# Sums over features in quarters of the array's columns, and layer 0's broadcast on ScalarE, in a four-layer graph network

## The chip, the cores and the metric

The kernel runs on one core of a Trainium2 chip. The metric is the device time of one execution in microseconds (us), as the median of several runs. The profile is of one further execution. Five engines work side by side: TensorE multiplies matrices (the profile shows its matmuls as PE and its weight loads as PEld), VectorE (DVE), ScalarE (ACT) and GpSimd (POOL) work elementwise, and SyncE (SP) starts most transfers.

## The reference, cut to what matters

The input x has 128 graphs of 64 nodes with 256 features. Four layers follow one another, each a graph operation, then a residual and a layer norm over the features:

```python
x = _layernorm(x + _L0_gnn_ref(x, adj, W, a))             # attention over all pairs of nodes
x = _layernorm(x + _L1_gnn_ref(x, ..., src, dst))         # attention over 512 listed edges
x = _layernorm(x + _L2_gnn_ref(x, adj, ...))              # neighbours' mean, two matmuls, batch norms
x = _layernorm(x + _L3_gnn_ref(x, adj, ...))              # two graph convolutions, four LSTMs
```

The change concerns layers 0 and 1. Layer 0 computes for each pair of nodes e = s1[i] + s2[j], leaky ReLU, a mask, softmax, and a product with Wh. Layer 1 is:

```python
Xq = (H @ W_lin.T).reshape(bt, n, h, dh)                  # 4 heads of 64 features
e = jnp.einsum('behd,hd->beh', leaky_relu(Xq[:, src] + Xq[:, dst], 0.2), a)
e = e + jnp.log(A0[src, dst] + EPS)
m = segment_max(e, src); ex = exp(e - m[src]); attn = ex / segment_sum(ex, src)[src]
Y = segment_sum(attn * Xv[:, dst], src) @ W_out.T
```

For every graph, edge and head, the sum over 64 features of a times a leaky ReLU is the heavy part: 128 x 512 x 256 values go through it. The kernel writes the leaky ReLU as a linear part and a plain ReLU, and folds the absolute value of a into the weights, so that only the sign of a is left to be applied after the ReLU.

## The kernel before, in words

Nodes are taken 512 at a time in 16 blocks q, each of four chunks c of 128 rows, which is two graphs (halves s) per chunk. A step b of a block, of which there are eight, is one graph: b = 2c + s. Two blocks share one softmax S (BPS = 2): 16 graphs with 4 heads give 64 rows of 512 edges.

`l1_graph(q, b)` gathers with a matmul: z, two chunks k of 128 features by 512 edges, is the sum of the queries at an edge's two ends. ScalarE makes u = ReLU(z) (line 324). An order of features was chosen in which feature p of chunk 0 and feature p of chunk 1 belong to the same head; line 325 on VectorE adds the second to the first, times `same`, the product of their signs. `reduce_heads` (line 312) then sums over the 128 partitions: its weights, cut out of `apad`, are zero but for four columns, which hold the signs of the four heads; where the cut begins decides which four of the 128 rows of the PSUM bank e receive this graph. All other rows get zeros added. A list `pend` keeps two steps between ReLU and sum.

`l1_softmax(S)` adds the linear part (line 335, weights `spads`) and the logarithm, and finds maxima and sums over edges with the same source by scans along the edges, which are sorted: a scan to the right and one to the left, the larger of the two, exponential, again two scans. TensorE transposes the result, GpSimd scatters it with four indirect transfers into a table in HBM (line 363), and SyncE loads it back as dense matrices, `ld` (line 369). `v_a` copies it into `am` on GpSimd (line 377) and multiplies it with the values v in 64x64 pieces (line 384); `v_b` applies W_out, the residual and the layer norm; `v_c` multiplies by the normalised adjacency, the start of layer 2.

Layer 0 is `l0_a` (transposes), `l0_b` (matmul with W and with two columns for s1 and s2, then the broadcast `sb` of s2 on GpSimd, line 227), `l0_c` (transposes of `sb`, lines 233 to 247), `l0_d` and `l0_e`.

The written order is one loop over q and b: each step runs `l1_graph` and then pieces of other blocks from a table `between`, layer 0 two blocks ahead (q + 2) and the values three behind (`LAG`). It is no final order: the framework is a planner, which goes by dependences, priorities in written order and its own costs, and may put an instruction of a later step ahead on an engine's queue. On the engine the queue is then followed in order. A tile with `bufs=n` has n buffers, and its writer waits until the readers of the oldest are done. PSUM has eight banks: two z of two banks each, one e, three m for everything else.

After the loop come layer 2 (from line 649) and layer 3 with its LSTMs (from line 790). Of the edits, only the helper `layernorm` (lines 84 to 97) is used there.

Of the kernel before, what the change touches and what calls it, by code (L numbers as in the profile page):

```python
# [17 lines left out]
P = 128  # L18
NB = 128
N = 64  # L20
# [11 lines left out]
SROWS = BPS * GQ * HEADS  # L32
PAIRS = N * N
# [7 lines left out]
def kernel(ctx: ExitStack, tc: tile.TileContext, i, out):  # L41
# [42 lines left out]
    def layernorm(dst, src, n, engine):  # L84

        st = small.tile([P, n, 6], F32, name="ln_st", bufs=6)
        mv = small.tile([P, n, 2], F32, name="ln_mv", bufs=6)
        ng = small.tile([P, n], F32, name="ln_ng", bufs=6)
        rs = small.tile([P, n], F32, name="ln_rs", bufs=6)
        for r in range(n):  # L90
            nc.vector.bn_stats(st[:, r, :], src[:, r, :])
            nc.vector.bn_aggr(mv[:, r, :], st[:, r, :])
        rsqrt(rs, mv[:, :, 1], n)
        nc.vector.tensor_scalar_mul(ng, mv[:, :, 0], -1.0)  # L94
        for r in range(n):
            engine.tensor_scalar(dst[:, r, :], src[:, r, :], ng[:, r:r + 1], rs[:, r:r + 1],
                                 op0=OP.add, op1=OP.mult)
# [13 lines left out]
    with ExitStack() as two:  # L111
# [52 lines left out]
        for k in range(KD):  # L164
            for m in range(KD):
                nc.scalar.dma_start(
                    wq[:, k, m * P:(m + 1) * P].rearrange("p (h j) -> p h j", h=HEADS),
                    i["W_linT"][k * P:(k + 1) * P].rearrange("p (h m j) -> p m h j", h=HEADS, m=KD)[:, m])
        aL1 = su.tile([P, D], F32, name="aL1")
        for m in range(KD):  # L170
            nc.scalar.dma_start(aL1[:, m * P:(m + 1) * P].rearrange("p (h j) -> p h j", h=HEADS),
                              i["L1_gnn_a"].rearrange("h (m j) -> m h j", m=KD)[m].partition_broadcast(P))
# [4 lines left out]
        apad = wa.tile([P, 2 * P - HEADS], F32, name="apad")  # L177
        same = wa.tile([P, 1], F32, name="same")
# [37 lines left out]
        def l0_b(q):  # L216
            xT = L0[q]["xT"]
            wh = L0[q]["wh"] = own(q, [P, PQ, D + 2], "wh")
            for c in range(PQ):
                p_ = bank([D + 2])  # L220
                for k in range(KD):
                    nc.tensor.matmul(p_, xT[:, k, c * P:(c + 1) * P], w0[:, k, :],  # L222
                                     start=k == 0, stop=k == KD - 1)
                nc.scalar.activation(wh[:, c, :], p_, AF.Copy)

            sb = L0[q]["sb"] = own(q, [P, PQ, P], "sb")
            nc.gpsimd.tensor_copy(sb, wh[:, :, D + 1:].to_broadcast([P, PQ, P]))

        def l0_c(q):
            wh, sb = L0[q]["wh"], L0[q]["sb"]  # L230
            sc = bank([PQ, P])
            for c in range(PQ):
                nc.tensor.transpose(sc[:, c, :], sb[:, c, :], ident)
            t = own(q, [P, PQ, P], "lr")
            for c in range(PQ):
                nc.vector.scalar_tensor_tensor(t[:, c, :], sc[:, c, :], wh[:, c, D:D + 1], mask,
                                               op0=OP.add, op1=OP.add)
            e = L0[q]["e"] = work.tile([P, PQ, P], F32, name="e0")
            nc.vector.scalar_tensor_tensor(e, t, SLOPE, t, op0=OP.mult, op1=OP.max)
            mx = small.tile([P, PQ], F32, name="mx")  # L240
            nc.vector.tensor_reduce(mx, e, AX.X, OP.max, negate=True)
            sm = small.tile([P, PQ], F32, name="sm")
            for c in range(PQ):
                nc.scalar.activation(e[:, c, :], e[:, c, :], AF.Exp, bias=mx[:, c:c + 1],
                                     accum_out=sm[:, c:c + 1])
            ri = L0[q]["ri"] = small.tile([P, PQ], F32, name="ri")
            nc.vector.reciprocal(ri, sm)
# [32 lines left out]
        def l1_qv(q, c2):  # L280
            xT, v = L1[q]["xT"], L1[q]["v"]
            sp = spads[q // BPS % 2].rearrange("p (s b c h) -> p s b c h", s=4, b=BPS, c=PQ)
            pv = bank([2, D])
            for c in (2 * c2, 2 * c2 + 1):
                pq = bank([D + HEADS])
                for k in range(KD):
                    nc.tensor.matmul(pq, xT[:, k, c * P:(c + 1) * P], wq[:, k, :],  # L287
                                     start=k == 0, stop=k == KD - 1)
                for k in range(KD):
                    nc.tensor.matmul(pv[:, c % 2, :], xT[:, k, c * P:(c + 1) * P], wv[:, k, :],  # L290
                                     start=k == 0, stop=k == KD - 1)

                qs = work.tile([P, 2, D], F32R, name="qs", bufs=6)
                L1[q]["qs"].append(qs)
                for s in range(2):
                    r, ro = slice(s * N, (s + 1) * N), slice((1 - s) * N, (2 - s) * N)
                    nc.scalar.activation(qs[r, s, :], pq[r, :D], AF.Copy)  # L297
                    nc.vector.tensor_sub(qs[ro, s, :], pq[r, :D], qs[r, s, :].bitcast(F32))  # L298
                    nc.scalar.activation(sp[r, s, q % BPS, c, :], pq[r, D:], AF.Copy, scale=SLOPE)
# [5 lines left out]
        def reduce_heads(q, b, t):  # L305
            S = q // BPS
            c, s = divmod(b, 2)
            r0 = ((s * BPS + q % BPS) * PQ + c) * HEADS
            first = q % BPS == 0 and b == 0
            if first:  # L310
                pes[S] = bank([E], name="e", bufs=1)
            nc.tensor.matmul(pes[S], apad[:, P - HEADS - r0:2 * P - HEADS - r0], t, start=first, stop=False)  # L312

        def l1_graph(q, b):

# [5 lines left out]
            u = work.tile([P, KD, E], F32, name="u", bufs=4)  # L323
            nc.scalar.activation(u, z, AF.Relu)  # L324
            nc.vector.scalar_tensor_tensor(u[:, 0, :], u[:, 1, :], same, u[:, 0, :], op0=OP.mult, op1=OP.add)  # L325
            pend.append((q, b, u[:, 0, :]))
            if len(pend) > DEEP:
                reduce_heads(*pend.pop(0))

        ld = {}  # L330

        def l1_softmax(S):
# [7 lines left out]
            nc.vector.tensor_tensor_scan(up, seg[:, :E], e, NEG, OP.add, OP.max)  # L340
            nc.vector.tensor_tensor_scan(dn[:, ::-1], seg[:, 1:][:, ::-1], e[:, ::-1], NEG, OP.add, OP.max)
            nc.vector.tensor_max(up, up, dn)
            nc.vector.tensor_sub(e, e, up)
            nc.scalar.activation(e, e, AF.Exp)


            nc.vector.tensor_tensor_scan(up, keep, e, 0.0, OP.mult, OP.add)
# [9 lines left out]
            nc.vector.reciprocal(rd, rows[1][:, :, :SROWS])  # L357
            for c in range(EC):
                nc.vector.scalar_tensor_tensor(at[:, c, :], rows[0][:, c, :SROWS], count[:, c:c + 1], rd[:, c, :],
                                               op0=OP.mult, op1=OP.mult)  # L360
# [11 lines left out]
        def v_a(q):  # L372
            S, b = divmod(q, BPS)
            v = L1[q]["v"]
            am = vp.tile([P, PQ * HEADS, N], F32, name="am", bufs=2)
            w = PQ * HEADS
            nc.gpsimd.tensor_copy(am, ld[S][:, :, b * w:(b + 1) * w].rearrange("p n r -> p r n"))
            pY = [bank([KD, PQ, N]) for _ in range(2)]
            for c in range(PQ):
                for h in range(HEADS):  # L380
                    for s in range(2):
# [3 lines left out]
                                         am[r, c * HEADS + h, :], start=True, stop=True)  # L385
# [4 lines left out]
        def v_b(q):  # L390
# [10 lines left out]
            x2 = L1[q]["x2"] = vp.tile([P, PQ, D], F32, name="x2")  # L401
# [81 lines left out]
        acol = su.tile([P, KD], F32, name="acol")  # L483

        def setup_queries():

            tmp2 = su.tile([P, KD, D], F32, name="tmp2")
            nc.vector.tensor_mul(tmp2, wq[:, :, :D], aL1[:, None, :].to_broadcast([P, KD, D]))
            for k in range(KD):
                nc.vector.reduce_sum(wq[:, k, D:], tmp2[:, k, :].rearrange("p (m h j) -> p h m j", m=KD, h=HEADS),  # L490
                                     axis=AX.XY)
            for m in range(KD):
                nc.vector.tensor_mul(tmp2[:, m, :P], aL1[:, m * P:(m + 1) * P], ident)
                nc.vector.reduce_sum(acol[:, m:m + 1], tmp2[:, m, :P], axis=AX.X)
# [4 lines left out]
        def setup_signs():  # L499

            nc.vector.tensor_scalar(acol, acol, 0.0, -2.0, op0=OP.is_lt, op1=OP.mult)
            nc.vector.tensor_scalar_add(acol, acol, 1.0)
            nc.vector.tensor_mul(same, acol[:, 0:1], acol[:, 1:2])
            nc.vector.tensor_scalar_mul(apad, iota_e[:, :2 * P - HEADS], 0.0)
            for h in range(HEADS):
                r, c0 = slice(h * 32, (h + 1) * 32), P - HEADS + h
                nc.vector.tensor_copy(apad[r, c0:c0 + 1], acol[r, 0:1])
# [115 lines left out]
        for q in range(NQ):  # L623
# [11 lines left out]
            for b in range(GQ):  # L635
                some(l1_graph, q, b)
                if q and q % BPS == 0 and b == DEEP - 1:
                    l1_softmax(q // BPS - 1)
# [4 lines left out]
        while pend:  # L643
            reduce_heads(*pend.pop(0))
        l1_softmax(NQ // BPS - 1)
        ph.close()

# [405 lines left out]
```

## Time and profile before

| | us |
|---|---|
| median of 3 runs | 2236.68 (2236.19 to 2237.63) |
| span of the profiled execution | 2237.3 |
| TensorE matmuls busy | 2163.4 |
| TensorE weight loads busy | 1411.7 |
| VectorE busy | 926.0 |
| ScalarE busy | 944.6 |
| GpSimd busy | 435.0 |

The page gives the busy time of each engine, the same in 40 slices of 55.9 us as digits (9 means 90% or more), the chain of work that ended last, and groups of instructions by line: tiles, shape, count, busy time, mean of one in ns, and the idle time ahead of them with what ended it. The busy time of a group counts overlapping instructions once, and matmuls overlap, since one begins while the one before drains. The start-to-start distance tells what a matmul costs. Line 312 appears as 256 instructions for 128 matmuls, because an fp32 matmul is two. Granted clock of TensorE in this execution: 0.991.

### The profile page before, as it was taken

What the parts mean: (1) busy time and instruction counts of PE and PEld (TensorE: products, weight loads), DVE (VectorE), ACT (ScalarE), POOL (GpSimd) and SP (SyncE); (2) the same over time, 40 slices, a digit from 0 to 9 for tenths busy, and PEclk for the clock granted to TensorE, in tenths of its full rate; (3) what the DMA queues carried; (4) which work ended last, traced back from release to release, by engine and by line L of the source; (5) the groups of instructions that cost most, each with busy time, mean ns of one, the idle gap of its engine ahead of it and who ended that gap; (6) DMA issues with size and microseconds to landing.
All of it is one profiled execution on the core that took longest, in us unless ns stands there. A gap on an engine that the chain in (4) does not pass through costs nothing.

```text
span 2237.3 us, 27559 instructions
## 1 busy us (share of the span) xinstructions
PE 2163.4 (97%) x10675; PEld 1411.7 (63%) x10675; DVE 926.0 (41%) x2136; ACT 944.6 (42%) x1821; POOL 435.0 (19%) x561
## 2 busy tenths in 40 slices
PE   5989999999899998999999999999999999999998
PEld 4667676666554444468468468468468468568467
DVE  7576756666544435232232323323323323323212
ACT  2655665656334802343343333333433433433333
POOL 1133334333320002011111111112112112112002
PEclk8999999999999998999999999999999999999999
DMA  4021233202223003000000000001001001000001
GB/s 121 19 40 29 50 50 51 50 32 39 41 41 111 19 0 104 0 20 29 29 20 29 29 19 29 29 20 29 29 19 29 28 20 29 19 10 29 10 0 29
DMA packets 129266, 74.46 MB, mean 33 GB/s; under 512 B 84976, under 2 KB 119920, under 8 KB 128880
## 3 DMA queue, kind: packets, MB, share of 16 engines
q1 hardware_dynamic: 124528, 70.74, 13.0%
q8 instruction: 84, 1.38, 0.3%
q10 hardware_dynamic: 3584, 0.92, 0.2%
q0 software_dynamic: 1024, 1.05, 0.2%
q14 instruction: 46, 0.38, 0.1%
HBM read 44.12 MB, written 28.57 MB: 32 GB/s over the span
## 4 chain that ended last, share of the span: by engine, by line
PE 81%; DVE 9%; ACT 5%; POOL 2%; DMA 1%; issue 1%; ACTq 0%; SPq 0%; POOLq 0%; DVEq 0%
PE l L927 34%; PE l L933 19%; PE pz L749 5%; PE pz L684 4%; DVE u L325 3%; PE g L867 2%; PE g L879 2%; PE e L312 2%; PE m L287 2%; PE m L222 2%; PE m L398 1%; PE g L829 1%; ACT u L324 1%; PE m L410 1%; PE m L290 1%
## 5 line engine op out<-in xcount | busy, mean ns | idle before, releaser
L927 PE MATMUL l<-H,wih 128*128 128x256 f32 (+2 forms) x2496 | 792.7, 470 | 0.8 <-ACT gate_g L947 0.5
L927 PEld LDWEIGHTS l<-H,wih 128*128 128x128 f32 x2496 | 467.7, 190 | 273.7 <-issue 179.4
L933 PE MATMUL l<-hid,whh 128*128 128x256 f32 (+2 forms) x1536 | 435.9, 437 | 0.0
L933 PEld LDWEIGHTS l<-hid,whh 128*128 128x128 f32 x1536 | 291.9, 190 | 128.4 <-issue 61.2
L939 ACT ACTIVATE gate_i<-l,bias 128x256 f32<-128x256 f32 (+2 forms) x176 | 100.0, 568 | 522.7 <-PE l L933 468.7
L942 DVE TENSOR_TENSOR gate_i<-gate_i,gate_g 128x256 f32<-128x256 f32 (+2 forms) x96 | 47.8, 498 | 580.8 <-ACT gate_g L939 580.8
L943 POOL TENSOR_TENSOR cell<-gate_f,cell 128x256 f32<-128x256 f32 (+2 forms) x96 | 83.6, 871 | 903.8 <-ACT gate_f L939 903.8
L82 POOL TENSOR_TENSOR ln_rs<-ln_rs,mhalf 128x2 f32<-128x2 f32 (+2 forms) x97 | 79.5, 819 | 498.7 <-DVE ln_ng L94 497.6
L324 ACT ACTIVATE u<-z 128x1024 f32<-128x1024 f32 x128 | 129.5, 1024 | 59.4 <-PE z L322 58.8
L312 PE MATMUL e<-u,apad 128*128 128x512 f32 x256 | 133.1, 606 | 11.3 <-DVE u L325 9.9
L939 ACT ACTIVATE gate_g<-l,bias 128x256 f32<-128x256 f32 (+2 forms) x176 | 100.1, 569 | 99.1 <-PE l L927 49.9
L325 DVE SCALAR_TENSOR_TENSOR u<-u,same 128x512 f32<-128x512 f32 x128 | 106.3, 841 | 57.8 <-ACT u L324 56.9
L939 ACT ACTIVATE gate_o<-l,bias 128x256 f32<-128x256 f32 (+2 forms) x176 | 99.2, 564 | 64.1 <-PE l L933 54.1
L946 DVE TENSOR_TENSOR cell<-gate_i,gate_g 128x512 f32<-128x512 f32 (+2 forms) x80 | 48.3, 603 | 156.1 <-ACT gate_g L939 155.6
L947 ACT ACTIVATE gate_g<-cell 128x256 f32<-128x256 f32 (+2 forms) x176 | 89.9, 511 | 52.9 <-DVE cell L946 38.4
L684 PE MATMUL pz<-A,w 128*128 128x512 f32 x256 | 112.1, 594 | 0.0
L322 PE MATMUL z<-gath_r,qs 128*128 128x512 f32 x256 | 106.9, 499 | 0.5 <-DVE qs L298 0.3
L684 PEld LDWEIGHTS pz<-A,w 128*128 128x128 f32 x256 | 48.1, 190 | 56.4 <-issue 54.3
L952 DVE TENSOR_TENSOR H<-gate_o,gate_g 128x512 f32<-128x512 f32 (+1 forms) x64 | 40.9, 639 | 89.0 <-PE l L927 71.4
L298 DVE TENSOR_TENSOR qs<-m,qs 64x256 fp32r<-64x256 f32 x128 | 54.1, 423 | 54.9 <-ACT qs L297 53.3
L939 ACT ACTIVATE gate_f<-l,bias 128x256 f32<-128x256 f32 (+2 forms) x96 | 51.0, 531 | 59.7 <-PE l L933 59.7
L287 PE MATMUL m<-wq,tT 128*128 128x260 f32 x256 | 71.2, 396 | 3.7 <-ACT tT L202 3.2
(240 smaller groups left out, 2674.8 us busy)
## 6 DMA issues: line engine op xcount, KB each, us to landing
xin<-in_x SPq DMA_DIRECT2D x16, 512.0 KB
ld<-table SPq DMA_DIRECT2D x16, 512.0 KB
x_dram<-x SPq DMA_DIRECT2D x16, 512.0 KB
x2r<-x_dram SPq DMA_DIRECT2D x32, 256.0 KB
x_dram<-A SPq DMA_DIRECT2D x64, 128.0 KB
x3r<-x_dram SPq DMA_DIRECT2D x64, 128.0 KB
out<-st SPq DMA_DIRECT2D x64, 128.0 KB
wih<-in_WihT SPq DMA_DIRECT2D x3, 1024.0 KB
```

Source lines behind the costliest of these rows:

```text
L287: nc.tensor.matmul(pq, xT[:, k, c * P:(c + 1) * P], wq[:, k, :], start=k == 0, stop=k == KD - 1)
L312: nc.tensor.matmul(pes[S], apad[:, P - HEADS - r0:2 * P - HEADS - r0], t, start=first, stop=False)
L322: nc.tensor.matmul(z[:, k, :], L1[q]["qs"][c][:, s, k * P:(k + 1) * P], gath_r, start=True, stop=True)
L324: nc.scalar.activation(u, z, AF.Relu)
L325: nc.vector.scalar_tensor_tensor(u[:, 0, :], u[:, 1, :], same, u[:, 0, :], op0=OP.mult, op1=OP.add)
L684: nc.tensor.matmul(p_, w1[:, k, m * P:(m + 1) * P], A[:, q, k * QT:(k + 1) * QT], start=k == 0, stop=k == KD - 1)
L749: nc.tensor.matmul(p_, w2[:, k, m * P:(m + 1) * P], hidden(q, k), start=k == 0, stop=k == M1 - 1)
L927: nc.tensor.matmul(gates[n], wih[p][:, k, mw * P:(mw + 1) * P], Hw[:, k, :, s, :], start=k == 0, stop=not s and k == KD - 1)
L933: nc.tensor.matmul(gates[n], whh[p][:, k, m * P:(m + 1) * P], hid[:, k], start=False, stop=k == KD - 1)
L939: nc.scalar.activation(act[n], gates[n], AF.Tanh if n == "g" else AF.Sigmoid, bias=bias[:, p - 1, m:m + 1])
L943: nc.gpsimd.tensor_tensor(cell[:, j], act["f"], cell[:, j], OP.mult)
L947: nc.scalar.activation(act["g"], cell[:, j], AF.Tanh)
```

## The change

Six edits are made.

1. The sum over features takes both chunks k on TensorE, so `same` and line 325 go, and the features stay in their natural order (the four strided loads of `wq` and two of `aL1` become one each). The weights in `apad` are now 32 columns wide (CG) and there is one set per chunk. Each matmul writes to 32 partitions of e only, a quarter of the columns of the array. Graphs are summed in fours, whose quarters n differ, in the order chunk, then the four from the youngest to the oldest. It is meant to let four sums run beside one another in four parts of the array.
2. The broadcast of s2 in layer 0 goes from GpSimd to ScalarE, and e of layer 0 is worked in place.
3. In softmax, the scan to the left runs over the result of the scan to the right, so that the maximum of the two is no longer needed, and the second half (sums, transposes, table) is a function of its own that is called one step later.
4. The layer norm subtracts the mean instead of adding its negative.
5. The rows of e have another order, by quarter, then softmax half; unused rows lie between them, and the reads of softmax, table and `am` follow it.
6. Buffers: u has 7 instead of 4, `am` 1 instead of 2, x2 shares the tile of y.

The core of the diff:

```diff
         for r in range(n):
-            engine.tensor_scalar(dst[:, r, :], src[:, r, :], ng[:, r:r + 1], rs[:, r:r + 1],
-                                 op0=OP.add, op1=OP.mult)
+            engine.tensor_scalar(dst[:, r, :], src[:, r, :], mv[:, r, 0:1], rs[:, r:r + 1],
+                                 op0=OP.subtract, op1=OP.mult)
...
-            nc.gpsimd.tensor_copy(sb, wh[:, :, D + 1:].to_broadcast([P, PQ, P]))
+            nc.scalar.activation(sb, wh[:, :, D + 1:].to_broadcast([P, PQ, P]), AF.Copy)
...
-        def reduce_heads(q, b, t):
+        def reduce_heads(four):
+            q, b, _ = four[0]
             S = q // BPS
...
-            nc.tensor.matmul(pes[S], apad[:, P - HEADS - r0:2 * P - HEADS - r0], t, start=first, stop=False)
+            for k in range(KD):
+                for q, b, u in reversed(four):
+                    n, r0 = b % 2 * 2 + b // 2 % 2, (q % BPS * 2 + b // 4) * HEADS
+                    nc.tensor.matmul(pes[S][n * CG:(n + 1) * CG, :],
+                                     apad[:, k, CG - HEADS - r0:2 * CG - HEADS - r0], u[:, k, :],
+                                     start=r0 == 0 and k == 0, stop=False)
...
-            u = work.tile([P, KD, E], F32, name="u", bufs=4)
+            u = work.tile([P, KD, E], F32, name="u", bufs=7)
             nc.scalar.activation(u, z, AF.Relu)
-            nc.vector.scalar_tensor_tensor(u[:, 0, :], u[:, 1, :], same, u[:, 0, :], op0=OP.mult, op1=OP.add)
-            pend.append((q, b, u[:, 0, :]))
-            if len(pend) > DEEP:
-                reduce_heads(*pend.pop(0))
+            pend.append((q, b, u))
+            if len(pend) == 4 + DEEP:
+                reduce_heads([pend.pop(0) for _ in range(4)])
...
             nc.vector.tensor_tensor_scan(up, seg[:, :E], e, NEG, OP.add, OP.max)
-            nc.vector.tensor_tensor_scan(dn[:, ::-1], seg[:, 1:][:, ::-1], e[:, ::-1], NEG, OP.add, OP.max)
-            nc.vector.tensor_max(up, up, dn)
-            nc.vector.tensor_sub(e, e, up)
+            nc.vector.tensor_tensor_scan(dn[:, ::-1], seg[:, 1:][:, ::-1], up[:, ::-1], NEG, OP.add, OP.max)
+            nc.vector.tensor_sub(e, e, dn)
             nc.scalar.activation(e, e, AF.Exp)
+            sm[S] = e, up, dn
+
+        def l1_weights(S):
+            e, up, dn = sm.pop(S)
...
-                if q and q % BPS == 0 and b == DEEP - 1:
-                    l1_softmax(q // BPS - 1)
+                if q and q % BPS == 0 and b in (DEEP - 1, DEEP):
+                    (l1_softmax, l1_weights)[b - DEEP + 1](q // BPS - 1)
...
-        while pend:
-            reduce_heads(*pend.pop(0))
+        reduce_heads(pend)
         l1_softmax(NQ // BPS - 1)
+        l1_weights(NQ // BPS - 1)
```

## The prediction

> **What bounds the kernel now.** I read the page first (busy rows and slices), then the groups, then single stretches of the timeline. The first 600 us hold the stages that the edits touch; after about 680 us nothing edited runs except the layer norm helper.
>
> ```profile
> PE 2163.4 (97%) x10675; PEld 1411.7 (63%) x10675; DVE 926.0 (41%) x2136; ACT 944.6 (42%) x1821; POOL 435.0 (19%) x561
> ...
> PE   5989999999899998999999999999999999999998
> ...
> L324 ACT ACTIVATE u<-z 128x1024 f32<-128x1024 f32 x128 | 129.5, 1024 | 59.4 <-PE z L322 58.8
> L312 PE MATMUL e<-u,apad 128*128 128x512 f32 x256 | 133.1, 606 | 11.3 <-DVE u L325 9.9
> ...
> L325 DVE SCALAR_TENSOR_TENSOR u<-u,same 128x512 f32<-128x512 f32 x128 | 106.3, 841 | 57.8 <-ACT u L324 56.9
> ```
>
> See that TensorE is the busy engine nearly everywhere, and that the pair of lines to be changed (L312 on TensorE, L325 on VectorE) holds 133 us and 106 us of busy time. The durations of matmuls overlap, so I count starts instead. In the chain, 128 fp32 instructions of 512 columns take 54.94 us, 0.429 us each:
>
> ```profile
> 684.11 54.94 PE pz L684 x128
> ```
>
> and in the timeline, where graph steps follow one another with nothing between:
>
> ```profile
> 583.24 1.03 PE L322 MATMUL z<-gath_r,qs 128*128 128x512 f32 x2
> 584.11 1.02 PE L312 MATMUL e<-u,apad 128*128 128x512 f32 x2
> 584.56 1.03 PE L322 MATMUL z<-gath_r,qs 128*128 128x512 f32 x2
> ...
> 589.90 1.12 PE L312 MATMUL e<-u,apad 128*128 128x512 f32 x2 [0.81 <-DVE u L325]
> ```
>
> A step takes 1.32 us from z to z: 0.86 for the two instructions of e, so 0.46 for the two of z.
>
> Two blocks q (one softmax) repeat every 70.8 us in the middle of the stage:
>
> ```profile
> 261.40:332.20 70.80, 68.41 (x428) 49.93 (x427) 46.94 (x111) 42.92 (x95) 26.04 (x28) 1.00 0.27 47
> ```
>
> The columns are TensorE, weight loads, VectorE, ScalarE, GpSimd, granted clock, DMA. Of the 428 matmuls, 32 are e (32 x 0.429 = 13.7 us). Counting all others at 0.429 us per 512 fp32 columns (transposes of 128 at the 0.109 us between their starts, z at 0.46 a pair) gives 51.6 us. So TensorE streams for 65.3 us and truly stalls for about 5.5 us: the stage is TensorE-bound, and ScalarE (43) and VectorE (47) have room.
>
> What it waits for between 100 and 600 us, in the waits view:
>
> ```profile
> PEld e L312 <- DVE u L325: 20.4, 26, 3.5
> PEld m L233 <- POOL sb L227: 10.2, 11, 2.6
> PEld m L353 <- DVE dn L348: 7.6, 7, 1.2
> PEld e L312 <- DVE e L337: 4.1, 7, 1.0
> ```
>
> All four are waits that the edits touch.
>
> **What the Trainium skill says.** "TensorEngine Tiling (Array Packing)", Key Properties: tiles "can execute LdWeights and Matmul in parallel", and a change of tiling mode drains TensorE. "TensorE: Matmul & The Clock Gate", Measured speedup vs the span model: three tiles of 32 columns with 512 moving columns ran 2.38 times as fast, within about 5 ns of the model of concurrent tiles. No 32-column tile is in this trace; the nearest thing is the 64x64 matmuls of L384, and they agree:
>
> ```profile
> 306.25 0.38 PE L222 MATMUL m<-w,tT 128*128 128x258 f32 x1
> 306.56 1.16 PE L384 MATMUL m<-am,v 64*64 64x64 f32 x64
> 307.65 0.50 PE L322 MATMUL z<-gath_r,qs 128*128 128x512 f32 x1
> ```
>
> Sixty-four fp32 instructions of 218 ns in 1.16 us are (1.16 - 0.22)/63 = 15 ns apart. One after the other they would be 0.429 x 64/512 = 54 ns apart: 3.6 of 4 tiles run at once, although each matmul is two instructions on the same tile. The drain: the last 128-wide stream ends at about 306.47 (306.25 + 0.22), z really begins at about 307.75 (its record is 0.10 longer than usual), so 1.28 us for 16 x 0.054 = 0.86: some 0.4 us per burst.
>
> **The change part by part.**
>
> (1) Column quarters. Before: 128 matmuls, 256 instructions, 256 x 0.429 = 109.8 us. After: 32 calls of 8 matmuls, 16 instructions each. With four tiles at once, 4 x 0.429 = 1.72 us plus 0.4 us of mode change = 2.12 us a call, 67.8 us in all: **42 us less** on the bounding engine. Bounds: perfect without drain 54.9 (55 less); no concurrency 32 x (6.86 + 0.4) = 232 us (123 more). I take four at once, because L384 shows it in this kernel.
>
> (2) L325 goes: 106 us of VectorE. It is off the path where TensorE is busy, and on it in two places. Near a softmax the scans of 1.2 us stand ahead of it on VectorE's queue and e waits; at the end of the loop (588 to 593 us) two of them take 4.2 us and TensorE waits some 3 us. e now waits for ScalarE's ReLU alone, still two steps old when it is used, and the call takes the youngest of its four first, so one wait serves all. The bank of e is next written four steps later than now, so its wait for L337 ends. I count **1 us in each of 7 softmaxes and 3 us at the end: 10 us**.
>
> (3) Layer 0's broadcast moves from GpSimd (0.61 us, behind whatever GpSimd waits for) to ScalarE directly behind the copies that it reads: 16 x 0.6 = 10 us for an engine busy 43 of 70.8 us. The transposes L233 wait 10.2 us for it in 11 cases, partly hidden by the preceding matmul's stream; I take **3 us**.
>
> (4) Softmax: one maximum (0.68 us of VectorE x 8) goes; the second scan now runs over the result of the first. The second half is emitted one step later, so TensorE's transposes L353 stand behind more work and the 1 us each that they wait (7.6 in 7) is covered: **up to 7 us, I take 3**. What waits instead is the table's round trip, treated below.
>
> (5) The negated mean (L94, 0.17 us) goes from every layer norm; GpSimd's power waits for it. Where TensorE is bound this is hidden by its queue; the last normalisation is exposed: 0.2 us, nothing. Layer 0's e in place, x2 in y and one am buffer: hidden by TensorE's work, as a block lies between two uses.
>
> (6) Start: six strided weight loads on ScalarE's queue become two. ScalarE's first copy now waits for these issues until 8.8 us; TensorE's L222 starts at 10.77 but needs VectorE's L419 (to 10.25), so that alone is worth 0.5. VectorE idles 1.9 us for aL1 at 12.9 and then runs without a gap to about 26, with four operations (0.29, 0.28, 0.55, 0.27 us) that go: **3 us** of 60.
>
> Sum: 42 + 10 + 3 + 3 + 3 = 61, less 3 us because ScalarE's copies meet the ReLUs of back-to-back steps (a step would be 0.46 + 0.53 = 0.99 us on TensorE, under ReLU's 1.02, so ScalarE limits these stretches): **58 us**. 2236.7 - 58 = **2179 us**.
>
> **The rivals.**
>
> *Round trip of the table, 2204.* The add of softmax starts at 266.27; the first am of GpSimd ends at 302.9, 36.6 us later; TensorE uses it at 306.56. GpSimd already waits:
>
> ```profile
> POOL am L377 <- DMA ld<-table: 63.6, 7, 11.7
> ```
>
> If the 70.8 us shrink by 6.6, TensorE arrives 36.5 us after the add instead of 40.3. The chain loses 0.7 (maximum) and some five L325 of 0.75, to 32 us, but the later second half can add l0_b, v_a and a step (about 6 us): 38, or 42.6 without that relief. So the table is 1.5 to 6 us late, 3.6 in the middle, in 7 pairs: +25. For it: the slack is small. Against: VectorE is freer, and the written order is only a wish, since the planner already runs graph steps ahead while a softmax is under way (z and e by turns from 263 to 275 us).
>
> *Nearly all stalls go, 2158.* The 5.5 us per pair fall to 2.3 instead of the 3.9 that the sum above leaves (13 us in 8 pairs), and of the drain 0.25 us hides behind weight loads (32 x 0.25 = 8 us): -21. For it: freer VectorE. Against: waits move to other engines rather than vanish.
>
> *Tiles overlap by halves only, 2247.* If the first instruction of a tile waits behind both of the tile before, 8 matmuls take 9 slots: 9 x 0.429 + 0.4 = 4.26 us a call, 136 in all, +27, less 16 from (2) to (6): +11. Against: L384's 15 ns. *No overlap at all, 2343:* +123 - 16. For both: four tiles share all 128 rows here, while the 64x64 ones share only halves.
>
> **How the numbers follow.** Forecast 0.62, round trip 0.15, stalls gone 0.12, halves 0.06, no overlap 0.05. The range 2156 to 2207 holds the first three with the unknown sizes in them (drain 0.2 to 0.5 us a call, stalls) and leaves out most of the last two. Faster 0.89, same 0.01, slower 0.10.
>
> **What would show it.** Right: L312's successor has 512 instructions whose starts come in fours a few ns apart, groups 0.43 us apart; the pair of blocks takes about 64 us; waits of e are on ScalarE's u, small; VectorE about 110 us less; layer 2 begins about 57 us earlier and everything after 700 us is unchanged. Wrong: starts 0.43 us apart singly or in twos; GpSimd's wait for ld showing up as TensorE's wait for am; ScalarE full in the loop.

## The result and the profile after

The changed kernel takes 2257.74 us (median, 2255.42 to 2259.17), the kernel before 2236.76 beside it: a ratio of 1.0092 with a 95% interval of 1.0075 to 1.011. It is **slower by 0.9%**, where 2.6% faster was forecast. The profiled execution has a span of 2253.6 us.

Start with two lines of the page of the changed kernel: busy time of the engines, and the shares of the chain of work that ended last.

```profile
PE 2143.3 (95%) x10931; PEld 1388.0 (62%) x10931; DVE 812.4 (36%) x1898; ACT 952.4 (42%) x1837; POOL 568.7 (25%) x545
...
PE 74%; issue 10%; POOL 9%; DVE 4%; ACT 2%; DMA 1%; POOLq 0%; SPq 0%; ACTq 0%; DVEq 0%
```

VectorE lost 113.6 us of busy time, about what was forecast. The surprise is GpSimd: it should have lost the broadcast of layer 0 and gained nothing, and its busy time rose from 435.0 to 568.7 us. It is only 25% busy, yet the chain runs through it for 9% of the span. Its groups on the page say why:

```profile
L95 POOL TENSOR_SCALAR A<-xin,ln_mv,ln_rs 128x256 f32<-128x256 f32 x64 | 82.1, 1292 | 1.7
...
L95 POOL TENSOR_SCALAR A<-x2r,ln_mv,ln_rs 128x256 f32<-128x256 f32 x64 | 77.8, 1225 | 3.3
L95 POOL TENSOR_SCALAR y<-y,ln_mv,ln_rs 128x256 f32<-128x256 f32 x64 | 77.5, 1220 | 1.7
```

These are three of the four layer norms, 64 normalisations each: layer 0's, the one at the end of layer 2, and layer 1's. One normalisation takes 1.22 us and more (second number after the bar). The first two of these groups in the kernel before:

```profile
L96 POOL TENSOR_SCALAR A<-xin,ln_ng,ln_rs 128x256 f32<-128x256 f32 x64 | 64.2, 1016 | 1.7
L96 POOL TENSOR_SCALAR A<-x2r,ln_ng,ln_rs 128x256 f32<-128x256 f32 x64 | 38.1, 605 | 3.3
```

Layer 1's group has 588 ns there. Layer 0's mean of 1016 ns mixes two lengths: four of its normalisations in a row took 6.01 us at 266.51 us and 2.16 us at 306.91. What makes some of them slow in the kernel before is not shown.

TensorE's sums, on the other hand, look as intended. The timeline of the changed kernel around one call:

```profile
306.63 1.92 PE L309 MATMUL e<-u,apad 128*32 128x512 f32 x16
308.48 0.74 PE L318 MATMUL z<-gath_r,qs 128*128 128x512 f32 x2
```

The z instructions are those of the next graph step. Sixteen instructions on tiles of 32 columns lie in 1.85 us from the start of e to the start of z. Their single starts come in fours 7 ns apart, at 306.63, 307.08, 307.51 and 307.94: four quarters run at once, each four 0.43 us after the one before.

Where the span went, by the times (us) at which stages begin in the traces. The third and fourth kernels are experiments from below: the changed kernel with the norm of before, and that one with the second half of softmax a step later.

| | before | after | norm of before | and softmax later |
|---|---|---|---|---|
| first graph step (z) | 54.5 | 49.3 | 49.3 | 49.0 |
| layer 2 begins | 599.2 | 580.2 | 553.9 | 543.1 |
| LSTMs begin | 884.9 | 879.5 | 839.7 | 828.8 |
| last input matmul of the LSTMs | 2223.6 | 2238.4 | 2178.4 | 2167.5 |
| end | 2237.3 | 2253.6 | 2192.2 | 2181.3 |
| layer 2 to the end | 1638.1 | 1673.4 | 1638.3 | 1638.2 |

Layers 0 and 1 became 19 us shorter, a third of the forecast, and everything after them became 35 us longer, though nothing but the layer norm was touched there.

### The profile page after: what moved, and what is told of

Read it like the earlier page. It is cut to its first block, busy times and chain, and to the rows that moved or that the text cites. A ratio compares the mean times of both kernels' runs of the same rounds, so it can differ in the third digit from the quotient of the medians.

```text
span 2253.6 us, 27724 instructions
## 1 busy us (share of the span) xinstructions
PE 2143.3 (95%) x10931; PEld 1388.0 (62%) x10931; DVE 812.4 (36%) x1898; ACT 952.4 (42%) x1837; POOL 568.7 (25%) x545
## 4 chain that ended last, share of the span: by engine, by line
PE 74%; issue 10%; POOL 9%; DVE 4%; ACT 2%; DMA 1%; POOLq 0%; SPq 0%; ACTq 0%; DVEq 0%
PE l L920 30%; PE l L926 18%; PE pz L742 5%; POOL A L95 3%; PE pz L677 3%; PE g L860 2%; PE g L872 2%; POOL y L95 2%; PE z L318 2%; PE e L309 2%; PE m L398 2%; POOL ln_rs L83 2%; PE m L281 1%; PE g L822 1%; PE m L284 1%
## 5 line engine op out<-in xcount | busy, mean ns | idle before, releaser
L920 PE MATMUL l<-H,wih 128*128 128x256 f32 (+2 forms) x2496 | 798.9, 473 | 0.8 <-ACT gate_g L940 0.5
L920 PEld LDWEIGHTS l<-H,wih 128*128 128x128 f32 x2496 | 470.0, 191 | 277.8 <-issue 183.5
L320 ACT ACTIVATE u<-z 128x1024 f32<-128x1024 f32 x128 | 128.6, 1024 | 34.7 <-PE z L318 34.1
L318 PE MATMUL z<-gath_r,qs 128*128 128x512 f32 x256 | 101.6, 478 | 4.9 <-ACT u L320 4.8
L95 POOL TENSOR_SCALAR A<-xin,ln_mv,ln_rs 128x256 f32<-128x256 f32 x64 | 82.1, 1292 | 1.7
L95 POOL TENSOR_SCALAR st<-x3r,ln_mv,ln_rs 128x256 f32<-128x256 f32 x64 | 77.9, 1226 | 3.4
L95 POOL TENSOR_SCALAR A<-x2r,ln_mv,ln_rs 128x256 f32<-128x256 f32 x64 | 77.8, 1225 | 3.3
L95 POOL TENSOR_SCALAR y<-y,ln_mv,ln_rs 128x256 f32<-128x256 f32 x64 | 77.5, 1220 | 1.7
```

What stands on the lines that cost most here:

```text
L95: engine.tensor_scalar(dst[:, r, :], src[:, r, :], mv[:, r, 0:1], rs[:, r:r + 1], op0=OP.subtract, op1=OP.mult)
L318: nc.tensor.matmul(z[:, k, :], L1[q]["qs"][c][:, s, k * P:(k + 1) * P], gath_r, start=True, stop=True)
L920: nc.tensor.matmul(gates[n], wih[p][:, k, mw * P:(mw + 1) * P], Hw[:, k, :, s, :], start=k == 0, stop=not s and k == KD - 1)
```

## The experiments

### Is it the norm? (four runs)

**The norm of before in the changed kernel** (ln_st gets four buffers instead of six, for room):

```diff
-        st = small.tile([P, n, 6], F32, name="ln_st", bufs=6)
+        st = small.tile([P, n, 6], F32, name="ln_st", bufs=4)
+        ng = small.tile([P, n], F32, name="ln_ng", bufs=6)
+        nc.vector.tensor_scalar_mul(ng, mv[:, :, 0], -1.0)
-            engine.tensor_scalar(..., mv[:, r, 0:1], rs[:, r:r + 1], op0=OP.subtract, op1=OP.mult)
+            engine.tensor_scalar(..., ng[:, r:r + 1], rs[:, r:r + 1], op0=OP.add, op1=OP.mult)
```

> The changed kernel with the layer norm of before (dense negated mean, add then multiply on GpSimd; statistics buffers 4 instead of 6 for room). Theory A, the norm is all of it: GpSimd's operation back from 1.22 to about 0.6 us, the time near the forecast, 2180 to 2195 us. Theory B, the norm costs only what is lost after 600 us (about 28 us of LSTMs, start of layer 3 and layer 2), and the other loss is the planner's order of the sums and the table's round trip: about 2230 us.

Measured: 2195.22 us (2194.0 to 2196.06), ratio to before 0.9804 (0.9788 to 0.982). With this one edit undone, the change is a gain of 2%.

**The norm of the change alone in the kernel before** (the same diff the other way round, nothing else):

> The kernel before with only the layer norm's edit. Theory A: slower by the 28 us seen after layer 1 plus what GpSimd loses in the first 600 us, 2265 to 2290 us; an LSTM group takes 174 instead of 170.4 us. Theory B: 2265 us, nearly all of it after 600 us. Third theory, the LSTM part is longer for another reason (order of the queues): 2237 us.

Measured: 2301.86 us (2299.67 to 2303.7), ratio 1.0277 (1.026 to 1.0295). So the edit costs 62.5 us in the changed kernel (2257.74 - 2195.22) and 63 in the one before (2301.86 - 2238.69).

The edit does two things: it subtracts instead of adding, and it reads the mean with a stride out of the pair (mean, variance) instead of from a dense tile. The next two runs separate them.

**Subtract, from a dense copy of the mean:**

```diff
+        nc.vector.tensor_copy(ng, mv[:, :, 0])
-            engine.tensor_scalar(..., mv[:, r, 0:1], rs[:, r:r + 1], op0=OP.subtract, op1=OP.mult)
+            engine.tensor_scalar(..., ng[:, r:r + 1], rs[:, r:r + 1], op0=OP.subtract, op1=OP.mult)
```

> As the changed kernel, subtract then multiply, but the mean is first copied to a dense tile. If the operation subtract is what takes 1.22 us on GpSimd, it stays 1.22 us and the time about 2258 us. If reading the mean with a stride of two elements is what costs, it takes 0.6 us and the time is that of the run with the add back.

Measured: 2260.09 us, ratio 1.0089 (1.0072 to 1.0106).

**Add, with the mean negated in place and read with a stride:**

```diff
+        nc.vector.tensor_scalar_mul(mv[:, :, 0], mv[:, :, 0], -1.0)
-            engine.tensor_scalar(..., mv[:, r, 0:1], rs[:, r:r + 1], op0=OP.subtract, op1=OP.mult)
+            engine.tensor_scalar(..., mv[:, r, 0:1], rs[:, r:r + 1], op0=OP.add, op1=OP.mult)
```

> As the changed kernel, but the mean is negated in place and added, read with a stride of two elements. If the operation subtract costs: 0.6 us each and the time of the run with the add back. If the stride costs: 1.22 us each and about 2258 us.

Measured: 2194.93 us, ratio 0.9803 (0.9786 to 0.9819). ln_st has its six buffers here, so their number doesn't matter either. One and the same group of GpSimd's normalisations from the first, third and fourth of these kernels:

```profile
L97 POOL TENSOR_SCALAR A<-x2r,ln_ng,ln_rs 128x256 f32<-128x256 f32 x64 | 38.2, 608 | 3.3
```
```profile
L97 POOL TENSOR_SCALAR A<-x2r,ln_ng,ln_rs 128x256 f32<-128x256 f32 x64 | 77.8, 1225 | 3.3
```
```profile
L96 POOL TENSOR_SCALAR A<-x2r,ln_mv,ln_rs 128x256 f32<-128x256 f32 x64 | 38.1, 605 | 3.3
```

Rows with the same tiles but another operation differ by a factor of two (608 and 1225 ns); rows with the same operation and another source of the mean don't (608 and 605; and 1225 dense against 1225 in the changed kernel). **It is the operation**, not the stride. In layer 0 the two operations differ less, 718 and 1292 ns. Why GpSimd takes longer to subtract, no run shows.

### How an idle engine costs 62 us

GpSimd waits far more than it works, so its longer instructions must stand in somebody's way. The chain of work of the changed kernel at the start of an LSTM group (start, length, what):

```profile
1229.08 0.73 POOL ln_rs L83
1229.89 2.43 POOL st L95 x2
...
1235.26 0.96 POOL A L95
1236.47 1.22 POOL A L95
...
1238.69 2.44 POOL A L95 x2
1241.17 0.46 PE g L822 x16
1241.63 7.04 PE l L920 x12
```

Three norms of two rows (st is the last norm of one group's output, A the norm at the end of layer 2, whose result is the input of the next group's graph convolution) go through GpSimd one behind the other, each with the power of its variance (`ln_rs`) ahead of it, and only then do the last of TensorE's matmuls of the graph convolution (L822), and behind them those of the gates (L920), start. The same chain for one whole group of the kernel with the norm of before, in its shares by line, is TensorE alone:

```profile
by line: PE l L922 56.4%; PE l L928 31.1%; PE g L874 4.1%; PE g L862 4.0%; PE g L824 2.6%; PE g L842 1.0%; PE g L971 1.0%
```

There nothing on GpSimd is in the chain. A group takes 170.4 us in the kernel before and in this one. In the changed kernel four groups take 174.4 us and one 172.7. In the group above TensorE waits for the norm twice (in brackets, us):

```profile
1239.97 0.46 PE L822 MATMUL g<-bdT,A 64*64 64x64 f32 x16 [1.07 <-POOL A L95]
1241.17 0.46 PE L822 MATMUL g<-bdT,A 64*64 64x64 f32 x16 [0.74 <-POOL A L95]
```

That is 1.8 of the 4 us. Nearly all the rest is TensorE's clock. In the next view the third number from the end is the granted clock, first behind these two waits, then at the same place in the group before:

```profile
1242.00:1245.40 3.40, 3.40 (x5) 1.35 (x4) 0.38 (x1) 0.70 (x2) 0.00 (x0) 0.50 0.36 114
1068.50:1071.90 3.40, 3.40 (x23) 1.75 (x24) 0.69 (x1) 1.28 (x2) 0.00 (x0) 1.00 0.35 116
```

For 3.4 us TensorE was granted half its clock, and the gates' matmuls start 0.853 us apart there instead of 0.429, so 1.7 us are lost. The group before has the same two waits (1.07 and 0.74 us) and the full clock behind them: it is the one with 172.7 us. Each of the four groups with 174.4 us has one such stretch. What decides which waits are followed by one is not shown.

The clock differs over the whole execution too. The granted clock is 0.979 in the changed kernel and 0.990 in the one with the norm of before. The part of the span that it leaves out is 47 us in the first and 22 in the second, so the slower clock is up to 25 of the 61 us between the two spans. It is an upper bound, since TensorE doesn't stream all of that time.

**The norms of this stage on VectorE, the subtraction kept** (the one at the end of layer 2 and the last), tests this part:

```diff
-            layernorm(x3, x, 2, nc.gpsimd)
+            layernorm(x3, x, 2, nc.vector)
...
-            layernorm(o[:, r], xr[:, r], len(cs), nc.gpsimd)
+            layernorm(o[:, r], xr[:, r], len(cs), nc.vector)
```

> The changed kernel, subtract kept, but the layer norms of layer 3 (in the graph convolutions and at the end) run on VectorE. Theory: the LSTM part loses because eight operations of 1.22 us stand one behind the other on GpSimd's queue before a graph convolution's matmuls, so an LSTM group goes back from 174.4 to about 170.4 us and the time to 2228 to 2232 us, still slow in the first 600 us. Rival: the subtract is slow on VectorE as well, or VectorE delays the LSTM's own work: no better than 2250 us.

Measured: 2231.62 us (2226.47 to 2234.12), ratio 0.9965 (0.9951 to 0.9979). The groups take 170.4 us again and 26 us come back; on VectorE the subtraction takes 0.41 us. Layer 2 still begins at 583.8 us: most of the rest of the loss lies in layers 0 and 1.

There the largest wait is for the copy `am`. GpSimd, then TensorE, in the timeline of the changed kernel:

```profile
286.50 4.85 POOL L95 TENSOR_SCALAR A<-xin,ln_mv,ln_rs 128x256 f32<-128x256 f32 x4
291.30 1.90 POOL L376 COPY am<-ld 128x1024 f32<-128x1024 f32 x1
```
```profile
286.06 3.75 PE L216 MATMUL m<-w,tT 128*128 128x258 f32 x16
293.25 1.03 PE L384 MATMUL m<-am,v 64*64 64x64 f32 x28 [3.44 <-POOL am L376]
```

The copy stands behind layer 0's norm on GpSimd's queue, and the norm takes 4.85 us, where it takes 2.17 in the kernel with the norm of before (at 277.05). TensorE reaches the values' matmuls (L384) and waits up to 3.4 us, five times. The waits between 100 and 540 us add up to 17.2 us for `am` in the changed kernel:

```profile
PE m L384 <- POOL am L376: 17.2, 5, 3.4
```

and to 3.8 in the kernel with the norm of before:

```profile
PE m L353 <- DVE dn L348: 10.2, 7, 1.7
PE m L386 <- POOL am L378: 3.8, 5, 0.8
...
PE m L353 <- ACT e L342: 3.6, 2, 2.7
```

These 13.4 us are half of the 26.3 by which layer 2 begins later (580.2 against 553.9 us). Some 10 more are the clock again: between 50 and 560 us the granted clock is 0.97 against 0.99, and the stretch from 293.1 to 296.5 us, right behind the wait shown, has 0.50. From layer 2 to the first LSTM matmul another 13.5 us are lost. TensorE waits there for the norms' outputs (`y` and `A`) too, but the parts of this stretch were not separated.

### Where the last 16 us are: the sums in whole bursts (three runs)

With the norm of before, 2195 us remain against a forecast of 2179. The planner puts other work between the eight matmuls of a call in 10 of the 32 calls: 48 stretches of L309 instead of 32, and a stretch of four instructions fills two quarters only. The first guess was that these pieces are what is missing. **Whole sums** (the norm of before from here on):

```diff
+            with tc.high_priority():
                 for k in range(KD):
                     for q, b, u in reversed(four):
```

> The run with the add back (2195.2 us beside 2238.7 before), with the eight matmuls of a sum given priority, so that the planner leaves them together: 32 bursts on TensorE instead of 48. Theory: a broken sum costs 1.5 us where its pieces of four instructions fill two quarters only (6 of them) and 0.35 us for each further change of mode, about 10 us in all: ratio to before 0.976, 2184 to 2187 us. Rival: a whole sum blocks TensorE's queue until the youngest u is there, and the time is the same, ratio 0.980.

Measured: 2217.09 us (2210.36 to 2217.98), ratio 0.9896 (0.988 to 0.9911): all 32 calls in one piece, and **22 us slower**. By the intervals between TensorE's starts, two pairs of blocks spend 14.8 us in the sums instead of 17.1, but TensorE now waits for `am`:

```profile
PE m L387 <- POOL am L379: 15.3, 5, 3.1
```

The copy stands behind layer 0's norm on GpSimd's queue in both kernels. But with priority a call of sums has left the place between layer 0's last product (L258) and the `am` matmuls, and TensorE arrives at them 6.9 us after the start of that product instead of 9.2. These waits are 11.5 us more than with broken sums, and the clock between 50 and 560 us is 0.97 instead of 0.99, some 10 us: together nearly the 24 us by which layer 2 begins later.

**Softmax in one part** on top of it:

```diff
-                if q and q % BPS == 0 and b in (DEEP - 1, DEEP):
-                    (l1_softmax, l1_weights)[b - DEEP + 1](q // BPS - 1)
+                if q and q % BPS == 0 and b == DEEP - 1:
+                    l1_softmax(q // BPS - 1)
+                    l1_weights(q // BPS - 1)
```

> As the run with whole sums, but the second half of softmax is called directly behind the first, as before. Theory of the forecast: the later second half covers waits of TensorE's transposes, so this is 2 to 7 us slower than the run with whole sums. Rival, the table's round trip: the later half makes the table late, so this is faster by up to 20 us.

Measured: 2197.22 us (2196.73 to 2199.33), ratio 0.9817 (0.9803 to 0.9831). The first copy `am` of a pair now stands before the norm on GpSimd's queue, and TensorE doesn't wait for it any more. The 20 us return, but no more. This kernel differs from the one with broken sums in two things, the sums and softmax, so what whole sums alone are worth is not shown; but without the pieces the 16 us are still missing.

**Tile by tile**, the loops over chunk and graph swapped in the kernel with whole sums:

```diff
-                for k in range(KD):
-                    for q, b, u in reversed(four):
+                for q, b, u in reversed(four):
+                    for k in range(KD):
```

> As the run with whole sums, but each graph's two chunks one after the other, so that four instructions in a row go to the same quarter of the columns. If TensorE starts matmuls for other quarters past waiting ones at any distance within the burst: no change to the run with whole sums. If it starts them strictly in order: 13 slots of 0.43 us instead of 4 per sum, 3.9 us x 32 = 124 us slower, about 2310 us. If it looks a few instructions ahead: between.

Measured: 2215.47 us (2212.14 to 2218.9), ratio 0.989 (0.9874 to 0.9906), the same as chunk by chunk. The starts still come in fours (us):

```
after:         306.628 .634 .641 .648   307.081 .088 .094 .101   307.510 ...
tile by tile:  242.205 .218 .231 .245   242.658 .671 .685 .698   243.087 ...
```

### Where the last 16 us are: queues (seven runs)

**Layer 0's norm on VectorE** takes it off GpSimd's queue, in three kernels: with broken sums, with whole sums, and with whole sums and softmax in one part.

```diff
-            layernorm(token_major(q), x, PQ, nc.gpsimd)
+            layernorm(token_major(q), x, PQ, nc.vector)
```

> The kernel with the adding norm (2195.2 us), with layer 0's norm on VectorE instead of GpSimd; the sums still break into pieces. Queue theory: what is left of TensorE's waits for am comes from the norm that stands ahead of the copy on GpSimd's queue; am then waits less, 2186 to 2192. Rival: VectorE is needed for the scans of softmax at the same time, the 64 normalisations (0.3 to 0.4 us each) delay them, and the time is 2195 to 2202.

> The kernel with whole sums and the softmax in two parts (2217.1 us), with layer 0's norm on VectorE. Queue theory: the 22 us that it is behind the kernel with broken sums are mostly the am copy behind layer 0's norm on GpSimd's queue (3.3 us a pair of blocks for TensorE); the norm gone from that queue, 2192 to 2202. Rival: the late second half of softmax costs by itself, since the table comes later whatever GpSimd does: 2212 to 2217, with TensorE's wait for am still about 3 us a pair.

> Whole sums, softmax in one part (2197.2 us), with layer 0's norm on VectorE. Queue theory: little, 2190 to 2197, since the am copy stands ahead of the norm there already. Rival: the freed GpSimd lets the remaining waits go and the unbroken sums bring their 10 us: 2180 to 2188. Other rival: VectorE's queue delays the scans, 2198 to 2205.

Measured: 2202.11 us (ratio 0.9837, 0.9824 to 0.9851), 2209.86 (0.9871, 0.9856 to 0.9887) and 2218.22 (0.991, 0.9895 to 0.9925). So +7, -7 and +21 us against the same kernels with the norm on GpSimd. In the kernel with whole sums and softmax in two parts, TensorE's wait for `am` fell from 15.3 to 4.2 us and the pair of blocks from 71.7 to 67.8 us in the middle of the stage: there the queue theory holds. But at the start, where VectorE prepares everything else, it costs: the graph steps of the second block begin at 86.3 instead of 76.5 us, and in the kernel with broken sums at 84.5 instead of 75.5. The last of the three has no `am` wait to lose, and only pays.

**The broadcast of layer 0 back on GpSimd**, in the kernel with broken sums:

```diff
-            nc.scalar.activation(sb, wh[:, :, D + 1:].to_broadcast([P, PQ, P]), AF.Copy)
+            nc.gpsimd.tensor_copy(sb, wh[:, :, D + 1:].to_broadcast([P, PQ, P]))
```

> The kernel with the adding norm (2195.2 us), with layer 0's broadcast back on GpSimd. Forecast's step: 3 us longer, about 2198, with TensorE's transposes waiting for sb some 10 us in all. Rival: ScalarE is nearer to full than GpSimd in this loop, and without the broadcast the ReLUs come earlier: 2190 to 2195.

Measured: 2197.5 us (2195.2 to 2200.62), ratio 0.9813 (0.98 to 0.9827). That is 2 us over 2195.2, and the intervals of the ratios overlap: the edit is worth about 2 us, not clear of noise.

What then was missing? The largest waits left in the list above are those of softmax's own transposes (m L353, for dn and for e), 13.8 us. The timeline of the kernel with the norm of before shows one:

```profile
312.78 0.74 PE L320 MATMUL z<-gath_r,qs 128*128 128x512 f32 x2
...
313.41 0.66 PE L353 MATMUL m<-ident,e 128*128 128x128 f32 x4
...
315.75 0.63 PE L353 MATMUL m<-ident,dn 128*128 128x128 f32 x4 [1.68 <-DVE dn L348]
```

Between the transposes of e and of dn lie a scan of 1.22 us on VectorE and nothing on TensorE, which follows its queue in order. **The second half of softmax one step later still** moves the transposes back in that queue:

```diff
-                if q and q % BPS == 0 and b in (DEEP - 1, DEEP):
-                    (l1_softmax, l1_weights)[b - DEEP + 1](q // BPS - 1)
+                if q and q % BPS == 0 and b in (DEEP - 1, DEEP + 1):
+                    (l1_softmax, l1_weights)[b // DEEP](q // BPS - 1)
```

> The kernel with the adding norm (2195.2 us), the second half of softmax called one step later still, which puts layer 0's transposes and one more graph step ahead of softmax's own transposes on TensorE's queue. Theory (softmax's transposes wait): TensorE's waits there, some 14 us between 100 and 540 us, fall to 3 or less, 2184 to 2189. Rival (the table is then late): the am copy waits for the transfer instead and takes it back, 2195 to 2205. Other rival: the sums and W_out's matmuls break into more pieces, each piece 0.35 us of mode change, and the gain is half of it, 2189 to 2195.

Measured: **2183.16 us** (2180.31 to 2185.97), ratio 0.9749 (0.9733 to 0.9765), the fastest of all. The same place in its timeline:

```profile
308.56 0.73 PE L320 MATMUL z<-gath_r,qs 128*128 128x512 f32 x2
309.85 0.66 PE L229 MATMUL m<-ident,sb 128*128 128x128 f32 x4 [0.55 <-ACT sb L223]
310.26 0.71 PE L320 MATMUL z<-gath_r,qs 128*128 128x512 f32 x2
310.81 0.60 PE L353 MATMUL m<-ident,e 128*128 128x128 f32 x4
311.52 0.63 PE L353 MATMUL m<-ident,dn 128*128 128x128 f32 x4
```

Layer 0's transposes (L229) and another graph step (L320) now fill the time of the scans. Between 100 and 540 us the wait for dn is 0.9 us instead of 10.2, and the one for `am` has not grown (3.3 us against 3.8): no cost of the later table is seen. The gain is not the clock: the whole executions have 0.991 and 0.990.

**Layer 0's norm on VectorE from block 4 on**, so that the start is spared, alone and together with the last edit:

```diff
-            layernorm(token_major(q), x, PQ, nc.gpsimd)
+            layernorm(token_major(q), x, PQ, nc.gpsimd if q < 4 else nc.vector)
```

> The kernel with the adding norm, layer 0's norm on VectorE from block 4 on and on GpSimd for the first four, which lie at the start of the stage. Theory (VectorE is short only at the start, GpSimd's queue matters in the middle): the pair of blocks takes 65.7 to 66.6 us as with all of it on VectorE, without the 10 us lost at the start, 2189 to 2193. Rival: the start was not the reason and VectorE delays softmax everywhere, 2196 to 2202.

> Both edits of the two runs before. Theory (both waits add up): 2179 to 2185, the forecast. Rival (they hide one another, or the table is late): not better than the better of the two alone, 2187 or more.

Measured: 2194.6 us (ratio 0.9802, 0.9788 to 0.9816) and 2186.97 (0.9769, 0.9754 to 0.9784). Alone it neither gains nor loses: the pair takes 65.7 us instead of 66.3 to 67.2, but around the switch block 5 begins 5 us later (210.5 against 205.5), so my claim that only the start suffers fell. Together they are not better than the later softmax alone; with the later softmax the wait for the copy was only 3.3 us to begin with.

## Why the prediction was wrong, by its steps

**The step that failed is (5)**: "The negated mean (L94, 0.17 us) goes from every layer norm; ... 0.2 us, nothing." It priced the instruction that goes and took the one that stays as unchanged. That one changes its operation on GpSimd, 256 times. In three of the four norms it goes from about 0.6 to 1.22 us, in layer 0's from 1.02 to 1.29. This costs 62.5 us, more than all the gains together: the waits of TensorE behind GpSimd's queue, and a lower granted clock beside them, which the prediction had not reckoned with either. The profile's groups don't name the operation of a TENSOR_SCALAR, the diff does, and its cost could have been bounded from both sides, as the prediction did for the column quarters; it was not seen as an unknown at all. A row of the kernel before, the product of two tensors of the same shape on GpSimd (`cell`, 0.87 us a piece), shows that an elementwise operation there can take 0.3 us longer than this one; 256 times that is an estimate of 77 us of GpSimd's time. None of the rivals held it either: those on the slow side doubted the tiles.

Step by step, by the sums of the intervals from one TensorE start to the next over two pairs of blocks (us; a stall counts for the line ahead of it):

| | before | after | norm of before | and softmax later |
|---|---|---|---|---|
| e, the sums | 27.1 | 17.1 | 17.1 | 15.2 |
| z | 23.9 | 24.0 | 22.3 | 24.4 |
| m<-w,tT, ahead of the am matmuls | 14.5 | 21.5 | 16.2 | 14.0 |
| softmax's transposes | 1.7 | 5.6 | 5.9 | 2.2 |
| all else | 74.5 | 72.3 | 71.9 | 72.7 |
| sum | 141.7 | 140.5 | 133.4 | 128.5 |

The second and third column hold one stretch of half clock each, 1.7 us; the others none.

(1) *Column quarters: right*, the size partly by luck. 17.1 us for 8 calls is 2.13 us each, where 2.12 was forecast. But this mean holds broken calls; a whole one takes 1.86 us (14.8 for 8 in the kernel with whole sums), and the pieces make up for the mode changes that were priced too high. Ten us less in two pairs is 40 in all, against 42. The statement of the Trainium skill in "TensorEngine Tiling (Array Packing)", Key Properties, that changing the mode drains TensorE, agrees in kind: by the starts around one burst, some 0.1 us are lost ahead of it and 0.2 behind it, against the 0.4 together taken from L384.

(2) *Waits of e: right.* TensorE's sums wait 1.6 us for u between 100 and 600 us, on ScalarE; in the kernel before it was 9.9 for u and 1.3 for the bank of e. The graph steps (z) now wait 4.8 us for ScalarE, where the forecast deducted 3.

(3) *Broadcast: 3 us forecast, about 2 measured* by putting it back, not clear of noise.

(4) *Softmax: wrong in sign.* Three us less were forecast; its transposes took 4 us more in two pairs. Between 100 and 540 us TensorE waits 10.2 us for dn, where it was 1.5 in the kernel before. Splitting softmax is not the reason: in the kernel with whole sums and softmax in one part it is 8.3. In the kernel before, the planner had put graph steps, z and e by turns, between the scans; with sums in fours there are fewer of them at hand. That this is the reason fits the order of the queue, but was not tested alone. One step later still, as the last column shows, the forecast's reasoning (more work ahead of the transposes) comes true; the emitted step had only not been late enough. That edit brought 12 of the 16 us left (2195.2 to 2183.2); of its 4.9 us in two pairs the transposes' lines are 3.7, and the shifts of the other lines add up to 1.2; the half clock, which begins at 382.2 us right behind a wait for dn, is 1.7 of the 4.9.

(6) *Start: 3 us forecast*, 5.2 measured at the first graph step.

*Everything after layer 2 unchanged* is right to 0.2 us for the kernel with the norm of before (1638.3 against 1638.1), and wrong by 35 us for the subtraction. In the kernel with both mends layer 2 begins 56.1 us earlier (57 forecast) and a pair takes 64.3 us (about 64 forecast).

The rival of the *round trip* named the right symptom, TensorE waiting for `am`. The cause was another: the transfer was in time, and the copy stood behind a norm. In the kernel with whole sums and softmax in two parts it is the same copy behind the same norm. *Halves* and *no overlap* fall with the starts 7 ns apart.

Of the 79 us between forecast and result, 62.5 are the subtraction, 12 came back with the later softmax, and 4 stay unexplained. Open is also why the kernels with whole sums are not faster: each came with another order of everything, and sums alone were not varied.

## What to carry to other kernels

A change of operation in an instruction is an edit with a price, even where shape, engine and count stay the same: find a row of that operation on that engine, or treat it as an unknown with two ends. An engine that is 20% busy can set the pace, if its queue holds what the busy engine needs next behind something slow. A short wait of TensorE can cost more than its length, so compare the granted clock of two runs before adding up waits. When an edit takes filler away from TensorE, look at what stood beside the waits before, and move the waiting work back by a step rather than only splitting it.

## What the runs showed of the hardware

- GpSimd's TENSOR_SCALAR on 128x256 f32 takes 1.22 us with subtract and multiply (1.22 to 1.25 in the kernel before with this norm) and 0.55 to 0.61 us with add and multiply, in three of the four norms; in layer 0's the means are 1.29 to 1.56 and 0.68 to 1.02 us. On VectorE subtract and multiply takes 0.41.
- Right behind waits of 1.07 and 0.74 us for GpSimd, TensorE's granted clock was 0.50 for 3.4 us in four LSTM groups, and its fp32 matmuls of 512 columns started 0.853 us apart instead of 0.429. Behind the same waits in another group it stayed at 1.00.
- Four fp32 tiles of 128 rows and 32 columns run fully side by side, 0.43 us for four instructions of 512 columns, though all share the 128 rows.
- The Trainium skill, "TensorE: Matmul & The Clock Gate", Part 3, The mechanism, says that matmuls keep program order in their starts. With the loops swapped, two matmuls of one quarter (four instructions) follow each other in the program; one after the other they would start 0.43 us apart. The records show fours 13 ns apart all the same, and the burst is as short (1.87 us to the next z). The measurement decides: instructions for other tiles passed waiting ones, if the planner kept the swapped order. The records don't name the quarter of an instruction; that the distance within a four doubled from 7 to 13 ns, as did the number of instructions in a row for one quarter, fits it.
